# Second attention: the maxima of a pair's second head come between the turning of the next queries' first head and that of their second

## Chip, core and metric

The kernel runs on one core of one Trainium2 chip. The metric is the device time of one execution, in microseconds (us). Twelve runs of the kernel before gave a median of 2171.01 us (2167.87 to 2173.53).

## What is computed

Two layers in sequence over x of 16 x 256 tokens by 256 features, float32, each step followed by a residual add and a layer norm: an RWKV-like attention, a quantised gated feed-forward, a latent attention with rotary positions (the "second attention"), and a mixture of 32 experts. The change lies in the second attention, of which this is the core:

```
cq = rms_norm(x @ w_qa.T, q_a_ln_w)
q = (cq @ w_qb.T)                      # 16 heads, 128 + 64 features; the 64 are rotated
ckv = x @ w_kva.T                      # shared latent keys and values
scores = einsum('bhqd,bhkd->bhqk', q_full, k_full) * scale
scores = where(causal, -inf, scores)
attn = softmax(scores, axis=-1)
out = einsum('bhqk,bhkd->bhqd', attn, v)
return out @ w_o.T
```

The mixture's router (scores, group choice, top 4 of 32, places in the experts' slots) is worked out inside the second attention's time, on the same engines.

## The kernel before, in words

The tokens are cut into 8 blocks of 512 (two sequences each). In the second attention (lines 1050 to 1340) each block b has 8 steps p, one for each pair of heads; n = 8b + p counts them. All engines follow the order in which the Python code issues instructions (`manual_schedule`): each engine has its own in-order queue, and an instruction waits on semaphores for what it reads and for the buffer that it overwrites.

One turn of the loop at line 1267 works on three pairs at once: pair n+2 is *asked* (its queries are projected and rotated), pair n+1 is *scored* (scores, softmax), and pair n-1 is *seen* (probabilities turned keys first, contexts). In the order of the code:

- scores of the scored pair's first head (line 1108, two sequences, TensorE), their maxima (`maxima`, line 1119, VectorE, from PSUM into `sm`), their exponentials (`exps`, line 1132, ScalarE);
- the reciprocal (line 1143, VectorE) and the scaling of the probabilities (line 1145, GpSimd) of the second head of the pair before it;
- `queries` (lines 1072 and 1078, TensorE): two PSUM tiles `q_ps`, one for each head of the asked pair;
- `first_place`: router parts of an earlier block (lines 888 to 997, VectorE above all) in steps 5, 6, 7 and 0, a layer norm's last part in step 3;
- reciprocal and scaling of the scored pair's first head; then `keys_first` of sequence 0 (line 1158, transposes on TensorE; line 1162, copies `aT` on ScalarE, which stand behind the exponentials in ScalarE's queue);
- `turn` for both heads of the asked pair (lines 1083 to 1091): three VectorE products out of `q_ps` (lines 1087, 1088, 1089) and a GpSimd addition (line 1090);
- a scatter of router rows (line 1004, GpSimd queue);
- scores of the scored pair's second head (TensorE), contexts of sequence 0 (line 1171), `keys_first` of sequence 1;
- the maxima of the scored pair's second head (VectorE);
- another scatter, then `second_place`: router parts (steps 3 to 7, 0 and 1), parts of the next block's latents (lines 672 to 746), and in steps 1, 2, 5 and 6 `output` (line 1190, TensorE, with the residual add of line 1198);
- the exponentials of the second head, contexts of sequence 1, the copy `cT` (line 1333), a last scatter.

Two pools of PSUM buffers matter. `ps_s` holds the scores in 2 buffers (tag "s"), so the first head's scores of the next turn need the buffers that the second head's maxima read. `ps_m` holds 3 buffers (tag "m") that go round in the order of allocation: in each turn the two `q_ps` first, then the tiles of `first_place` and `second_place` (`l_ps`, `n_ps`, `xT_ps`, `lat_ps`, `cqT_ps`, `kT_ps`, `o_ps`), so that the third tile behind a `q_ps` takes that `q_ps`'s buffer. `turned` goes round three buffers, one for each head.

Of the kernel before, what the change touches and what calls it, by code (L numbers as in the profile page):

```python
# [88 lines left out]
def seq_postln_kernel(ctx: ExitStack, tc: tile.TileContext, a: dict, out: bass.AP, cap: int):  # L89
# [80 lines left out]
    def layernorm(ys, dsts):  # L170
        normalize(ys, dsts, *moments(ys))
# [827 lines left out]
    def scatter(b, which):  # L999


        dest = dests[b]
        for t, k in [divmod(j, K) for j in which]:
            put = nc.gpsimd.indirect_dma_start(  # L1004
                out=xp_d[:, :],
                out_offset=bass.IndirectOffsetOnAxis(ap=dest[:, k, t : t + 1], axis=0),
                in_=xs[b][:, t, :],
                in_offset=None,
                bounds_check=slots - 1,
                oob_is_err=False,  # L1010
            )
            if scattered:
                tc.declare_no_dep(put.ins, group="scatter", reason="other rows")
            tc.add_to_no_dep_group("scatter", put.ins)
            scattered.append(put.ins)
# [34 lines left out]
    with ExitStack() as ph:  # L1050
# [16 lines left out]
        def queries(cqT, pair):  # L1067

            pss = []
            for k in range(2):  # L1070
                ps = ps_m.tile([P, BLK], F32, tag="m", name="q_ps")
                nc.tensor.matmul(  # L1072
                    ps, lhsT=w_q[:, 2 * pair + k, :], rhs=cqT[:, 0, :], start=True, stop=False
                )
                pss.append(ps)
            for k, ps in enumerate(pss):
                rows = slice(k * QR, (k + 1) * QR)
                nc.tensor.matmul(
                    ps, lhsT=w_qr[rows, pair, :], rhs=cqT[rows, 1, :], start=False, stop=True
                )  # L1080
            return pss

        def turn(ps, h):
            qT = pq.tile([P, BLK], F32, tag="qT", name="qT")
            qr = turned[h % 3]
            lo, hi = slice(KVLR, KVLR + HR), slice(KVLR + HR, P)
            nc.vector.tensor_tensor(qT, ps, cst["q_cos"], ALU.mult)  # L1087
            nc.vector.tensor_tensor(qr[lo, :], ps[hi, :], cst["q_sin"][hi, :], ALU.mult)  # L1088
            nc.vector.tensor_tensor(qr[hi, :], ps[lo, :], cst["q_sin"][lo, :], ALU.mult)  # L1089
            nc.gpsimd.tensor_tensor(qT, qT, qr, ALU.add)  # L1090
            return qT
# [60 lines left out]
        def keys_first(heads, s):  # L1152

            aTs = []
            for sm in heads:
                a_ps = ps_a.tile([P, 3 * P], F32, tag="a", name="a_ps")
                for i in range(3):
                    nc.tensor.transpose(  # L1158
                        a_ps[:, i * P : (i + 1) * P], sm.pr[:, s, i * P : (i + 1) * P], ident
                    )  # L1160
                aT = pa.tile([P, 3 * P], F32, tag="aT", name="aT")
                copy = nc.scalar.copy(aT, a_ps)  # L1162
                aTs.append(aT)
            return aTs, copy

        def contexts(c_ps, aTs, copy, kf, s):


            for i in range(2):
                for k, aT in enumerate(aTs):  # L1170
                    mm = nc.tensor.matmul(  # L1171
                        c_ps[k * KVLR : (k + 1) * KVLR, s, i * P :],
                        lhsT=kf[:, 2 * s + i, :KVLR],
                        rhs=aT[:, : 2 * P] if i == 0 else aT[:, 2 * P :],
                        start=(i == 0),
                        stop=(i == 1),
                    )
                    if i == k == 0:
                        after(mm.ins, copy.ins, "beside the other head's")
# [32 lines left out]
        def step_latents(b):  # L1212
            if b < NB:
                if b not in lats:
                    lats[b] = latents(b, ps_m, "m")
                next(lats[b], None)

        def step_route(b):
            if b >= 0:
                if b not in routes:  # L1220
                    routes[b] = route(b, ps_m, "m")
                next(routes[b], None)

        def first_place(b, p):
            last = b - 1
            if p == 3 and last >= 0:
                x = x_t[last * NTT : (last + 1) * NTT]
                normalize(x, x, *norms.pop(last), eng=nc.scalar)
            if p >= 5:
                step_route(last)  # L1230
            if p == 0:
                step_route(last - 1)
# [25 lines left out]
        def scatters(b, p):  # L1258

            lo = 3 * (p - 2)  # L1260
            return [(b, j) for j in range(max(lo, 0), min(lo + 3, GT * K))] if b >= 0 else []

        NS = NB * NP
        with tc.manual_schedule(engines=engines):
            qTs, sms = {}, {}
            step_latents(1)
            for n in range(-2, NS + 1):
                b, p = divmod(n, NP)
                todo = scatters(b - 2, p)

                def one_scatter():
                    if todo:
                        scatter(todo[0][0], [todo.pop(0)[1]])

                scored = n + 1 if 0 <= n + 1 < NS else None
                asked = n + 2 if 0 <= n + 2 < NS else None
                seen = n - 1 if 0 <= n - 1 < NS else None
                if scored is not None:
                    kT = latent[scored // NP][2]
                    heads = sms[scored] = [Softmax(), Softmax()]  # L1280
                    qT2 = qTs.pop(scored)
                    for s in range(2):
                        heads[0].scores(qT2[0], kT, s)
                        heads[0].maxima(s)
                        heads[0].exps(s)
                if n in sms:
                    sms[n][1].divide()
                if asked is not None:
                    q_ps = queries(latent[asked // NP][0], asked % NP)
                if n >= 0:  # L1290
                    first_place(b, p)
                elif n == -2:

                    for _ in range(3):
                        step_latents(1)
                if scored is not None:
                    heads[0].divide()
                if seen is not None:
                    pair = sms.pop(seen)
                    kf = latent[seen // NP][1]  # L1300
                    part, j = divmod(seen % NP, NP // 2)
                    if j == 0:
                        cT = cTs[seen // NP, part] = pc.tile(
                            [P, NP // 2, BLK], F32, tag="cT", name="cT"
                        )
                    c_ps = ps_c.tile([P, 2, S], F32, tag="c", name="c_ps")
                    aTs0 = keys_first(pair, 0)
                    if p == 4:
                        step_latents(b + 1)
                if asked is not None:  # L1310
                    qTs[asked] = [turn(ps, 2 * asked + k) for k, ps in enumerate(q_ps)]
                one_scatter()
                if scored is not None:
                    heads[1].scores(qT2[1], kT, 0)
                    heads[1].scores(qT2[1], kT, 1)
                if seen is not None:
                    contexts(c_ps, *aTs0, kf, 0)
                    aTs1 = keys_first(pair, 1)
                if scored is not None:
                    heads[1].maxima(0)  # L1320
                    heads[1].maxima(1)
                one_scatter()
                if n >= 0:
                    second_place(b, p)
                elif n == -1:
                    for _ in range(2):
                        step_latents(1)
                if scored is not None:
                    heads[1].exps(0)
                    heads[1].exps(1)  # L1330
                if seen is not None:
                    contexts(c_ps, *aTs1, kf, 1)
                    nc.scalar.copy(cT[:, j, :], c_ps.rearrange("p s t -> p (s t)"))
                one_scatter()
            step_route(NB - 2)
            last = NB - 1
            for s in range(2):
                output(last, 1, s)
            x = x_t[last * NTT :]
            layernorm(x, x)  # L1340
# [298 lines left out]
```

## Time and profile before

| what | value |
| --- | --- |
| median of 12 runs | 2171.01 us |
| profiled execution, its own time | 2173.98 us |
| profiled execution, span of instructions | 2172.2 us |
| mean granted TensorE clock | 0.985 |
| busy: TensorE products / VectorE / ScalarE / GpSimd | 2077.4 / 1560.4 / 762.3 / 897.7 us |
| second attention, from about 1128 to about 1890 us | |
| from 1500 to 1600 us: TensorE / VectorE / ScalarE / GpSimd busy | 96.79 / 85.64 / 60.54 / 66.91 us |
| one block in the steady part (step 1 of block 4 to step 1 of block 5) | 1529.19 to 1626.60 us |

The time of the profiled execution is 1.8 us above its span, and 3 us above the median. PE stands for TensorE's products, PEld for its weight loads, DVE for VectorE, ACT for ScalarE, POOL for GpSimd. A timeline row has the start, the time, the engine, the line, the operation, its tiles, and in brackets the idle time of the engine just before it and what ended it. A row of the chain of waits has a start, a time and the instruction that held the end at that moment.

### The profile page before, as it was taken

Reading aid. Unit: us, or ns where it says so; the run is one execution under the profiler, and the core shown is the slowest. Engines: PE = TensorE matmul, PEld = TensorE weight load, DVE = VectorE, ACT = ScalarE, POOL = GpSimd, SP = SyncE. Lnnn points to the kernel's source line nnn. Section 1 sums busy time; section 2 is a strip of 40 time slices with the busy share of each in tenths; the row PEclk is TensorE's granted clock in tenths of the full one; section 3 lists DMA queues with packets and bytes.
Section 4 is the critical chain, followed back from the end, with each engine's and each line's share of the span. In section 5 each row is a group of like instructions: output and inputs, shape, how many; then the busy total and the mean of one; then the engine's idle time right before and its main releaser. Section 6 shows DMA issues by size and latency. Waiting matters only on the chain.

```text
span 2172.2 us, 29585 instructions
## 1 busy us (share of the span) xinstructions
PE 2077.4 (96%) x9544; PEld 1449.7 (67%) x9544; DVE 1560.4 (72%) x3960; ACT 762.3 (35%) x2237; POOL 897.7 (41%) x972
## 2 busy tenths in 40 slices
PE   8999999999999999999998999999999999988887
PEld 5777777777777777565555666666666666656665
DVE  7888888888888887223346679888797978853436
ACT  2212121211112112212225565656666564522323
POOL 5623232323232322000015545757666675734556
PEclk9999999999999999999999999999999999989999
DMA  9544444444453231110000000000000000042337
GB/s 314 183 133 148 129 136 131 140 130 148 135 151 95 88 95 49 48 34 1 0 1 1 1 1 1 29 4 6 3 4 2 3 3 2 25 169 66 88 134 294
DMA packets 102042, 169.73 MB, mean 78 GB/s; under 512 B 17807, under 2 KB 67191, under 8 KB 99712
## 3 DMA queue, kind: packets, MB, share of 16 engines
q1 hardware_dynamic: 88000, 158.45, 23.1%
q0 software_dynamic: 9216, 5.19, 0.9%
q10 hardware_dynamic: 4672, 4.21, 0.6%
q8 instruction: 76, 1.25, 0.2%
q14 instruction: 78, 0.64, 0.1%
HBM read 128.75 MB, written 56.95 MB: 85 GB/s over the span
## 4 chain that ended last, share of the span: by engine, by line
PE 71%; DVE 18%; ACT 4%; issue 2%; POOL 2%; DMA 1%; another core or an unknown queue 1%; POOLq 0%; SPq 0%; DVEq 0%; ACTq 0%
PE p_ps L419 15%; PE o_ps L512 10%; PE v_ps L449 8%; PE g_ps L208 4%; PE u_ps L208 4%; PE s_ps L1108 4%; PE d_ps L247 3%; PE o_ps L1190 3%; PE q_ps L1072 3%; PE c_ps L1171 3%; DVE sm L1119 2%; PE a_ps L1158 2%; DVE turned L1089 2%; DVE qT L1087 2%; DVE turned L1088 2%
## 5 line engine op out<-in xcount | busy, mean ns | idle before, releaser
L499 POOL TENSOR_TENSOR wkv<-su,Wr_sb 128x512 f32<-128x512 f32 x128 | 160.2, 1273 | 503.2 <-PE p_ps L419 313.9
L1145 POOL TENSOR_TENSOR pr<-pr,rr 128x256 f32<-128x256 f32 (+1 forms) x256 | 206.9, 836 | 153.9 <-DVE rr L1143 127.2
L512 PE MATMUL o_ps<-w_o,wkv 128*128 128x256 f32 (+1 forms) x1024 | 251.6, 388 | 6.2 <-POOL wkv L499 5.8
L1132 ACT ACTIVATE pr<-sm,nm 128x128 f32<-128x128 f32 (+1 forms) x512 | 226.1, 444 | 77.7 <-DVE nm L1119 63.4
L449 PE MATMUL v_ps<-xm,w_Wv 128*128 128x512 f32 x512 | 242.5, 596 | 6.0 <-DVE xm L395 6.0
L512 PEld LDWEIGHTS o_ps<-w_o,wkv 128*128 128x128 f32 x1024 | 192.1, 190 | 75.8 <-POOL wkv L499 45.1
L1108 PE MATMUL s_ps<-kT,qT 128*128 128x128 f32 (+1 forms) x1024 | 199.2, 338 | 22.2 <-DVE nm L1119 22.1
L421 ACT COPY t_sb<-p_ps 128x256 f32<-128x256 f32 x128 | 47.4, 370 | 467.2 <-PE p_ps L419 465.9
L419 PE MATMUL p_ps<-xm,w_Wk 128*128 128x256 f32 x896 | 204.9, 380 | 1.5 <-DVE Wr_sb L424 1.5
L419 PEld LDWEIGHTS p_ps<-xm,w_Wk 128*128 128x128 f32 x896 | 170.8, 191 | 52.9 <-issue 27.8
L419 PE MATMUL p_ps<-xm,w_Wr 128*128 128x256 f32 x896 | 204.4, 379 | 0.7 <-POOL xm L401 0.5
L1090 POOL TENSOR_TENSOR qT<-qT,turned 128x512 f32<-128x512 f32 x128 | 162.8, 1274 | 89.1 <-DVE turned L1089 87.9
L419 PEld LDWEIGHTS p_ps<-xm,w_Wr 128*128 128x128 f32 x896 | 170.0, 190 | 25.2 <-DVE Wk_sb L424 0.9
L1108 PEld LDWEIGHTS s_ps<-kT,qT 128*128 128x128 f32 x1024 | 146.8, 194 | 43.1 <-issue 35.4
L1162 ACT COPY aT<-a_ps 128x384 f32<-128x384 f32 x256 | 109.9, 481 | 170.6 <-PE a_ps L1158 170.4
L470 DVE TENSOR_TENSOR_SCAN st<-decay,kv 128x255 f32<-128x255 f32 x256 | 163.9, 682 | 4.4
L1119 DVE CUSTOM_DVE_ANT_0 sm<-s_ps,const 128x128 f32<-128x128 f32 (+1 forms) x512 | 154.2, 354 | 14.6 <-PE s_ps L1108 11.6
L1004 POOL DMA_INDIRECT xp_d<-xs,dest x128 | 128.3, 1002 | 58.8 <-issue 31.6
L142 POOL TENSOR_TENSOR rstd<-rs_t,nhalf 128x4 f32<-128x4 f32 (+1 forms) x33 | 33.3, 1010 | 287.3 <-DVE rs_t L141 277.1
L494 ACT ACTIVATE Wr_sb<-Wr_sb 128x512 f32<-128x512 f32 x128 | 73.5, 621 | 217.9 <-DVE Wr_sb L427 188.7
L449 PEld LDWEIGHTS v_ps<-xm,w_Wv 128*128 128x128 f32 x512 | 97.7, 191 | 74.3 <-issue 61.3
L218 DVE TENSOR_TENSOR hT<-sg,u_ps 128x512 f32<-128x512 f32 x56 | 38.4, 687 | 147.4 <-PE u_ps L208 134.0
(189 smaller groups left out, 3765.1 us busy)
## 6 DMA issues: line engine op xcount, KB each, us to landing
w_Wk<-wsum_d SPq DMA_DIRECT2D x56, 448.0 KB
w_Wr<-wsum_d SPq DMA_DIRECT2D x56, 448.0 KB
w_Wv<-in_Wv_dram SPq DMA_DIRECT2D x64, 256.0 KB
res_d<-zeros SPq DMA_DIRECT2D x16, 1024.0 KB
res<-res_d SPq DMA_DIRECT2D x16, 1024.0 KB
w_e<-in_W_experts_dram SPq DMA_DIRECT2D x32, 384.0 KB
xp_d<-empty SPq DMA_DIRECT2D x4, 1360.0 KB
xe<-xp_d SPq DMA_DIRECT2D x32, 170.0 KB
```

The source lines that it names most:

```text
L208: mm = nc.tensor.matmul(ps, lhsT=w[:, c, i * P : (i + 1) * P], rhs=xT[:, c, :], start=(c == 0), stop=(c == DC - 1),)
L419: nc.tensor.matmul(to, lhsT=w[:, at, :], rhs=x[:, bt, :], start=True, stop=True)
L449: nc.tensor.matmul(ps, lhsT=self.w3["Wv"][:, 2 * h + c, :], rhs=self.xms["Wv"][:, 2 * c : 2 * c + 2, :].rearrange("p s t -> p (s t)"), sta ...
L470: nc.vector.tensor_tensor_scan(st[:, s, 1:], decay[:, n : n + 1].to_broadcast([P, S - 1]), kv[:, s, : S - 1], 0.0, ALU.mult, ALU.add,)
L499: nc.gpsimd.tensor_tensor(wkv, self.su[h], self.both(self.r, h), ALU.mult)
L512: nc.tensor.matmul(ps.rearrange("p t d -> p (t d)") if opens else ps[:, tt % 2, :], lhsT=self.wkv[h][:, tt * P : (tt + 1) * P], rhs=w_o[:, ...
L1004: put = nc.gpsimd.indirect_dma_start(out=xp_d[:, :], out_offset=bass.IndirectOffsetOnAxis(ap=dest[:, k, t : t + 1], axis=0), in_=xs[b][:, ...
L1090: nc.gpsimd.tensor_tensor(qT, qT, qr, ALU.add)
L1108: nc.tensor.matmul(ps[:, lo:hi], lhsT=qT[:, s * S + i * P : s * S + (i + 1) * P], rhs=kT[:, s * S : s * S + hi - lo], start=True, stop=True,)
L1119: nc.vector.tensor_tensor_reduce(out=sm[:, lo:hi], in0=self.ps[s][:, lo:hi], in1=cst["mask"][:, lo:hi], scale=-(DQ**-0.5), scalar=-MASKED, ...
L1132: nc.scalar.activation(self.pr[:, s, lo:hi], self.sm[s][:, lo:hi], AF.Exp, bias=self.nm[:, s, i : i + 1], scale=-1.0, accum_out=self.rs[:, ...
L1145: nc.gpsimd.tensor_tensor(self.pr[:, :, lo:hi], self.pr[:, :, lo:hi], rr[:, :, i : i + 1].to_broadcast([P, 2, hi - lo]), ALU.mult,)
```

## The change

In the turn of the loop, the second head of the asked pair is turned after the maxima of the scored pair's second head, where it was turned before them.

```diff
                 if asked is not None:
-                    qTs[asked] = [turn(ps, 2 * asked + k) for k, ps in enumerate(q_ps)]
+                    qTs[asked] = [turn(q_ps[0], 2 * asked)]
                 one_scatter()
                 if scored is not None:
                     heads[1].scores(qT2[1], kT, 0)
                     heads[1].scores(qT2[1], kT, 1)
                 if seen is not None:
                     contexts(c_ps, *aTs0, kf, 0)
                     aTs1 = keys_first(pair, 1)
+
                 if scored is not None:
                     heads[1].maxima(0)
                     heads[1].maxima(1)
+                if asked is not None:
+                    qTs[asked].append(turn(q_ps[1], 2 * asked + 1))
                 one_scatter()
```

No instruction is added or taken away. TensorE, ScalarE and SyncE keep their order. On VectorE the second head's lines 1087 to 1089 pass behind the four maxima (line 1119); on GpSimd the second head's addition (line 1090) passes behind one scatter (line 1004), in the steps that have one.

## Prediction

> **What bounds the kernel now.** I read the page first, then the sums by stretch, the waits of TensorE inside the second attention (1128 to 1890 us), the chain of waits over one steady block, and the timelines of the engines over that block. TensorE is busy 96.8% of the stretches from 1400 to 1800 us and VectorE 85.6%, so what TensorE waits for there is short:
>
> ```profile
> PE s_ps L1108 <- DVE nm L1119: 22.1, 14, 5.3
> PE c_ps L1171 <- ACT aT L1162: 9.1, 13, 0.8
> ```
>
> The columns are the total, the number of waits and the longest. The scores wait for the maxima that still read their buffer: that is the wait the change aims at. In a steady block it comes twice, in the turn's first scores of step 0 and of step 1:
>
> ```profile
> 1613.45 0.87 PE L1171 MATMUL c_ps<-aT,kf 128*64 128x256 f32 x8
> 1615.76 1.55 PE L1108 MATMUL s_ps<-kT,qT 128*128 128x128 f32 x8 [1.45 <-DVE nm L1119]
> ...
> 1626.60 1.55 PE L1108 MATMUL s_ps<-kT,qT 128*128 128x128 f32 x8 [0.91 <-DVE nm L1119]
> ```
>
> The chain of waits over the block says why: from step 4 on it holds nothing but VectorE rows, until the maxima let TensorE go.
>
> ```profile
> 1572.51 0.18 DVE rr L1143
> ...
> 1626.11 0.34 DVE sm L1119
> 1626.47 0.14 issue
> 1626.60 1.55 PE s_ps L1108 x8
> ```
>
> So from 1572.5 to 1626.5 VectorE sets the pace and never idles; afterwards TensorE does (steps 1 and 2), with a turn through ScalarE in step 3. An order that only shuffles VectorE's work gains at the one place where the chain leaves VectorE, and loses whatever makes VectorE's own work longer.
>
> **What moving the turn gains.** A turn is 0.71 us three times, 2.13 us (from 1623.68 to 1625.81). Behind the maxima it no longer delays the release of the scores' buffers: -2.13 us, once a block, at the exit in step 0. In steps 4 to 7 it gains nothing, because VectorE does the turn anyway before the next maxima.
>
> **What it costs on VectorE.** GpSimd's addition (line 1090, 1.27 us) starts 0.15 us behind its turn. Until now the second head's addition ran beside the maxima, which read one operand from PSUM and one from SBUF; after the change it runs beside the router's parts of `second_place`, whose products have both operands in SBUF. What that does shows in the rows:
>
> ```profile
> 1510.07 1.93 DVE L866 TENSOR_TENSOR eq<-left,top 128x128 f32<-128x128 f32 x1
> 1510.22 1.62 POOL L1145 TENSOR_TENSOR pr<-pr,rr 128x256 f32<-128x256 f32 x2
> ...
> 1537.97 1.28 POOL L1090 TENSOR_TENSOR qT<-qT,turned 128x512 f32<-128x512 f32 x1 [0.90 <-DVE turned L1089]
> 1538.97 0.31 DVE L984 COPY pos<-carry 128x32 f32<-128x32 f32 x1
> ...
> 1589.42 1.28 POOL L1090 TENSOR_TENSOR qT<-qT,turned 128x512 f32<-128x512 f32 x1 [0.86 <-DVE turned L1089]
> 1590.42 0.56 DVE L866 TENSOR_TENSOR gt<-gs 128x256 f32<-128x256 f32 x1
> ...
> 1595.45 1.66 POOL L1145 TENSOR_TENSOR pr<-pr,rr 128x256 f32<-128x256 f32 x2 [1.03 <-DVE top L952]
> 1595.47 0.73 DVE L866 TENSOR_TENSOR eq<-left,top 128x128 f32<-128x128 f32 x1
> 1596.24 1.01 DVE L866 TENSOR_TENSOR eq<-eq,const 128x128 f32<-128x128 f32 x1
> ```
>
> The comparison `eq`, 0.29 us at its quickest, takes 1.93, 0.73 or 1.01 us beside a GpSimd product, and always ends about 0.15 us behind it. The last two groups beside line 1090 show that the addition does the same: the copy and `gt` last until just behind its end. With T the end of the second turn, the addition holds VectorE's SBUF products until T + 1.42. Step by step:
> - Step 4: line 909 comes first, at T + 0.03, 0.12 us ahead of the addition. If it is held, it ends at T + 1.5 and not at T + 0.3: 1.2 us. If it gets through, the addition starts behind it and holds line 717 for about 0.25 us. Below these the bound is nothing. The nearest row is 1510.07, an operation 0.15 us ahead that was held: 1.2 us.
> - Step 5: `gt` ends at T + 1.7 where it would take 0.42 us: 1.23, less the 0.13 that it already loses: 1.1 us.
> - Steps 6 and 7: a reduction runs first (not held), then `eq` ends at T + 1.57 where it would end at T + 0.52: 1.05 us each.
> - Step 7 gets something back: the 1.93 us came with both halves of line 1145 back to back behind a scatter. VectorE being later, GpSimd is idle by then, and the pair becomes 0.73 + 1.01, as in step 6: -0.47 us.
>
> At the exit: 1.2 + 1.1 + 1.05 + 1.05 - 0.47 - 2.13 = +1.8 us. TensorE starts step 1 that much later, since the 2.36 us that it waited are all the slack it had.
>
> The Trainium skill, "SBUF — State Buffer", section "Who interferes with whom", says that a VectorE instruction with two SBUF inputs contends with a GpSimd one that reads SBUF, and that whichever issues first has the ports for its whole length. The second half speaks for line 909 in step 4, and the row at 1510.07 against it. By the rule step 4 costs 0.25 us, the exit comes at +0.85 us, and the whole sum is some 6 us smaller.
>
> **What it costs on TensorE.** The moved turn is also the last reader of the second `q_ps`, and its buffer of three comes back later by the maxima, 1.2 us.
> - Step 3: `lat_ps` is the third tile behind it and starts at 1565.92; the turn would end at 1566.35 where it ended at 1565.12. TensorE waits 0.46 us, and line 691, its reader, stands in the chain: +0.46 us.
> - Step 1: `o_ps` is the third tile (behind `n_ps` and `lat_ps`). Before, the turn ended at 1537.82 and `o_ps` started at 1538.60, one block later 1635.2 and 1636.0. Now VectorE enters the step with the turn of step 0 still to do (2.13) and two small copies held by its addition (0.35): its first maxima start at 1628.06 + 1.8 + 2.48 = 1632.3. From there to the reciprocal of line 1143 it is 2.27 us as before (ScalarE's exponentials); the copies `aT` stand behind these and end at 1635.45, 0.7 us after TensorE wants them. Turn, maxima, turn from 1634.7: 2.13 + 1.2 + 2.13, ends at 1640.15. `o_ps` arrives at 1636.0 + 1.8 + 0.7 = 1638.5 and waits for that: TensorE is now 4.15 us late. In step 2 VectorE's idle time (0.9, 0.95 and 2.79 us before) takes up its lag.
> - Step 0's first `q_ps` also waits for the turn of step 7, some 1.2 us, but the contexts behind it wait longer for `aT`: nothing more.
>
> ScalarE's exponentials of the second head are free sooner but stand behind the copies: nothing. The scatter that passes ahead, and the second query itself, used half a turn later, have some 5 us to spare: nothing.
>
> **The sum.** A block: 4.15 + 0.46 = 4.6 us. Blocks 1 to 5: 23.0. Block 6 (step 1 of block 7 has no `lat_ps`, so `o_ps` takes another buffer; TensorE waits there at a lower clock already): an estimate from the parts above, 0.46 + 1.5 = 2.0. Block 7 has only steps 4 and 5, partly hidden: 1.6. Block 0 has no router parts and TensorE sets its pace: nothing. In the very first turns the maxima release earlier (-2.13) but the addition now stands ahead of line 142 (+1.15): -1.0. Together +25.6 us: the span of the profiled execution would go from 2172.2 to 2197.8, and the median, 3 us below that execution's own time, from 2171.0 to 2196.6. With step 4 at 0.25 it is 2190.6.
>
> **Rivals.**
> - GpSimd's addition costs VectorE nothing (the moved pairs don't meet, or short operations slip through). Then the exit gains 2.13 us, but in step 1 the turn ends at 1635.95 whatever happened before, since the exponentials set it, and `o_ps` starts within 0.1 us of where it did: +0.4 a block with step 3. Blocks 1 to 5 give +2.0, block 6, without that wait, -4.5, the first turns -1: 2167.5 us. Against it: the rows above, in every block.
> - Faster, the other side: neither the addition nor the buffer of `q_ps` binds, and the waits for the maxima vanish: 22.1 us less the two of the first turns (5.3 and 2.85) is 13.95; the 3.1 us of the low clock behind the 1.86 us wait at 1810.58 (2.90 for 1.55, 3.62 for 1.88); and 1.0 at the start: -18, 2153 us. It decides if the second turn ends before the third tile behind `q_ps` is due in steps 1 and 3; now that margin is 0.8 us in both, and the turn moves by 1.2.
> - The new waits in steps 7 and 0 (up to 1.8 us at once) bring the low clock each block: in the stretch 1810 to 1818 us, behind waits of 0.68 and 1.86 us, the granted clock was 0.58; behind 1.45 us it stayed at 1.00. Six times 3.1 us on top: 2215 us.
> - That the order does not change can be left out: on VectorE and GpSimd it is as the diff says, on the other engines as before.
>
> **Numbers.** Forecast 0.68 (its own range 2180 to 2208), low clock 0.08, no cost beside the addition 0.14, faster 0.10. Slower by over 0.2% (2175.4 us; about what a measurement of this kernel can tell from no change): 0.76. The third case straddles the band: 0.10 within, 0.04 faster; with the last, faster 0.14. The range runs from 2163, which takes in the third case, to the low clock's 2215.
>
> **What would show it.** Right: `eq` of steps 6 and 7's `second_place` and `gt` of step 5 at 1.3 to 1.7 us beside line 1090; VectorE's waits unchanged but its busy time up by some 25 us; TensorE waiting at `o_ps` in step 1 and `lat_ps` in step 3 for line 1089; a block of about 102 us. Wrong: `eq` at 0.29 us there; or TensorE's first scores of step 1 earlier in the block than now; or a block of 95 us.

## The result and the profile after

The changed kernel takes 2189.49 us (median of 7 runs, 2187.05 to 2193.72) against 2169.75 us for the kernel before on the same chip (28 runs): a ratio of 1.0093, 95% interval 1.0084 to 1.0103, so +19.7 us. The forecast was 2196.6. The profiled execution of the changed kernel takes 2187.3 us, its span is 2185.5.

TensorE's order is the same in both kernels, so the two traces can be laid side by side, from step 1's first scores of one block to those of the next. A steady block takes 100.79 us after and 97.41 before: +3.38, where the forecast said +4.6. Taken by steps (from a step's first scores to those of the next), step 1 is 1.79 us longer, step 3 0.47, steps 4 to 0 together 1.12 (1.04 of it in step 0), and the others are the same. The attention's last contexts start 17.7 us later.

TensorE's waits inside the second attention, after (total, number, longest):

```profile
PE s_ps L1108 <- POOL qT L1090: 16.7, 9, 7.9
PE c_ps L1171 <- ACT aT L1162: 15.1, 25, 0.8
PE o_ps L1190 <- DVE turned L1089: 7.5, 5, 1.5
PE xT_ps L179 <- DVE turned L1089: 6.1, 5, 1.2
PE s_ps L1108 <- DVE nm L1119: 1.7, 1, 1.7
PE lat_ps L684 <- DVE turned L1089: 1.2, 6, 0.2
```

The wait for the maxima (nm), which the change aims at, has all but gone: 22.1 us became 1.7. Its place is taken by other waits for VectorE's turns (o_ps, xT_ps, lat_ps) and, in the scores themselves, by a wait for GpSimd's addition. The longest of these, 7.9 us, stands in the very first turns, where the maxima cost 5.3 and 2.9 us before. TensorE's timeline shows where in the block the others stand; the last row is from before, where o_ps came without a wait:

```profile
1725.76 0.66 PE L179 MATMUL xT_ps<-const,xs 128*128 128x128 f32 x4 [1.22 <-DVE turned L1089]
...
1727.19 1.58 PE L1108 MATMUL s_ps<-kT,qT 128*128 128x128 f32 x8
...
1739.07 1.58 PE L1108 MATMUL s_ps<-kT,qT 128*128 128x128 f32 x8 [0.94 <-POOL qT L1090]
...
1750.16 3.72 PE L1190 MATMUL o_ps<-w_ov,cT 128*128 128x256 f32 x16 [1.49 <-DVE turned L1089]
...
1636.01 3.62 PE L1190 MATMUL o_ps<-w_ov,cT 128*128 128x256 f32 x16
```

The first four are step 7, step 0's first scores (their wait of 1.45 us is gone), step 1's first scores and step 1's o_ps. The chain of waits no longer leaves VectorE at step 1's scores as it did before. It stays on VectorE, with one turn through ScalarE's exponentials, up to o_ps:

```profile
1740.88 1.05 DVE sel L973
...
1742.80 1.87 ACT pr L1132 x8
...
1749.42 0.70 DVE turned L1089
...
1750.16 3.72 PE o_ps L1190 x16
```

So whatever lengthens VectorE's work in steps 4 to 7 now also sets o_ps. And VectorE's work did get longer. The timeline of all engines, at the second turns of steps 4, 5 and 6 and at step 7's first part; the last two rows are from before, the same products of steps 5 and 7:

```profile
1689.36 0.23 DVE L909 TENSOR_SCALAR sco<-sco 128x128 f32<-128x128 f32 x1
1689.42 1.31 POOL L1090 TENSOR_TENSOR qT<-qT,turned 128x512 f32<-128x512 f32 x1 [0.51 <-DVE turned L1089]
...
1701.94 0.42 DVE L866 TENSOR_TENSOR gt<-gs 128x256 f32<-128x256 f32 x1
1702.06 1.43 POOL L1090 TENSOR_TENSOR qT<-qT,turned 128x512 f32<-128x512 f32 x1 [0.81 <-DVE turned L1089]
1702.28 1.49 DVE L866 TENSOR_TENSOR eq<-gs 128x256 f32<-128x256 f32 x1
...
1716.04 1.26 POOL L1090 TENSOR_TENSOR qT<-qT,turned 128x512 f32<-128x512 f32 x1 [0.82 <-DVE turned L1089]
1716.24 1.21 DVE L866 TENSOR_TENSOR eq<-left,top 128x128 f32<-128x128 f32 x1
...
1720.88 0.73 DVE L866 TENSOR_TENSOR eq<-left,top 128x128 f32<-128x128 f32 x1
1721.64 1.01 DVE L866 TENSOR_TENSOR eq<-eq,const 128x128 f32<-128x128 f32 x1
...
1688.31 0.41 DVE L866 TENSOR_TENSOR eq<-gs 128x256 f32<-128x256 f32 x1
1713.81 0.29 DVE L866 TENSOR_TENSOR eq<-left,top 128x128 f32<-128x128 f32 x1
```

A product out of two SBUF operands that is caught by the addition lasts until just behind the addition's end: `eq` 1.49 us where it took 0.41, and 1.21 where it takes 0.29. In the step 4 pair nothing is caught. To put a number on it, I add up in one block what VectorE's operations last over the shortest time of their kind in the steady blocks of all traces, as far as that is more than 0.1 us: 3.7 us before and 6.0 to 6.3 after.

### The profile page after: what moved, and what is told of

It is laid out like the page before. It is cut to its first block, busy times and chain, and to the rows that moved or that the text cites. A ratio compares the mean times of both kernels' runs of the same rounds, so it can differ in the third digit from the quotient of the medians.

```text
span 2185.5 us, 29567 instructions
## 1 busy us (share of the span) xinstructions
PE 2070.9 (95%) x9544; PEld 1441.6 (66%) x9544; DVE 1576.3 (72%) x3960; ACT 758.1 (35%) x2237; POOL 898.6 (41%) x972
## 4 chain that ended last, share of the span: by engine, by line
PE 67%; DVE 24%; issue 3%; ACT 3%; POOL 2%; another core or an unknown queue 1%; DMA 0%; POOLq 0%; DVEq 0%; ACTq 0%; SPq 0%
PE p_ps L419 15%; PE o_ps L512 10%; PE v_ps L449 8%; PE g_ps L208 4%; PE u_ps L208 4%; DVE sm L1119 3%; PE s_ps L1108 3%; PE d_ps L247 3%; PE o_ps L1190 3%; DVE eq L866 2%; DVE turned L1089 2%; DVE turned L1088 2%; PE c_ps L1171 2%; DVE qT L1087 2%; PE q_ps L1072 2%
## 5 line engine op out<-in xcount | busy, mean ns | idle before, releaser
L1108 PE MATMUL s_ps<-kT,qT 128*128 128x128 f32 (+1 forms) x1024 | 197.5, 336 | 18.4 <-POOL qT L1090 16.7
```

The source lines that it names most:

```text
L1108: nc.tensor.matmul(ps[:, lo:hi], lhsT=qT[:, s * S + i * P : s * S + (i + 1) * P], rhs=kT[:, s * S : s * S + hi - lo], start=True, stop=True,)
```

## The experiments

Two theories stood against each other in what follows. Theory 1: the late addition on GpSimd stands beside the router's products and lengthens VectorE's chain. Theory 2: the second q_ps's buffer comes back late, and TensorE waits for it at o_ps. The runs were made on several chips. They differ mainly behind the attention: from its last contexts to the end of the span it is 267 us in the trace of the changed kernel, 231 in b_late's. Each run is therefore compared with the kernel before on its own chip, and the steady block, which does not contain that part, is compared across all of them.

### The addition cut short, in the new order and in the old

```diff
-            nc.gpsimd.tensor_tensor(qT, qT, qr, ALU.add)
+            nc.gpsimd.tensor_tensor(qT[:, :cols], qT[:, :cols], qr[:, :cols], ALU.add)
...
-                    qTs[asked].append(turn(q_ps[1], 2 * asked + 1))
+                    qTs[asked].append(turn(q_ps[1], 2 * asked + 1, 16))
```

> The order of after, with the second head's addition on GpSimd (line 1090) cut from 512 columns to 16: it leaves the rotation's second part out of the other columns, so that GpSimd no longer holds VectorE's ports for 1.3 us behind the late turn, while the late turn itself and the late return of the second q_ps stay. Theory 1 (the addition beside the router's products is what costs): the 1.07 us of step 5 and the 0.93 us of steps 6 and 7 vanish, the time falls from 2189 to within 3 us of the kernel before or below it (2160 to 2173 us). Theory 2 (the late return of q_ps costs): o_ps in step 1 still waits for line 1089, and the time stays above 2182 us. If both share it: about 2175 to 2180 us.

> The control for the run before: the order of before, with the same addition cut to 16 columns (the same part of the rotation is left out). Beside the maxima the addition cost VectorE next to nothing, so both theories expect the time of before, 2166 to 2170 us; if it is far lower, the addition's length matters by itself (through the scores that wait for it), and the pair has to be read by its difference.

Both kernels leave the rotation's second part out of all but 16 columns of the second head. The new order came to 2130.59 us, the old one to 2126.40, before to 2131.12 on that chip: ratios of 0.9996 (0.9987 to 1.0005) and 0.9981 (0.9972 to 0.9990). A block takes 97.47 us in the new order and 96.46 in the old. Against the whole addition, the new order has lost 3.32 us a block and the old one 0.95. The control was expected to stay where it was and did not: beside the old neighbours the addition was not free either (in the control `gt` takes 0.42 us where it took 0.56 before, and the slow `eq` of step 7 takes 0.72 where it took 1.93), so the pair is read by its difference. The addition's length costs 2.4 us a block more in the new order than in the old. That is theory 1, but not all of it: with the addition short in both, the new order is still 1.0 us a block slower than the old, and o_ps in step 1 still waits 1.2 us for line 1089.

### The addition alone moved

```diff
+                if asked is not None:
+                    qT, qr = adds[0]
+                    add = nc.gpsimd.tensor_tensor(qT, qT, qr, ALU.add)
+                    if scored is not None:
+                        after(add.ins, last_max.ins, "behind the maxima")
```

> The order of before on VectorE and TensorE, both turns ahead of the maxima; only the second head's addition on GpSimd waits for the last maximum, so that it stands beside the router's products as in after. q_ps comes back as early as before, and the maxima release the scores' buffers as late as before. Theory 1: VectorE's chain from step 4 to step 0 grows by 1.07 + 0.93 + 0.93 us a block (and up to 0.7 more in step 7), about 3 us a block over six blocks: 2184 to 2192 us. Theory 2: nothing but the later second query, 2169 to 2174 us.

2152.58 us against 2131.12: a ratio of 1.0100 (1.0084 to 1.0115), +21.5 us, and a block of 99.92 us (+2.5). No VectorE or TensorE instruction has moved, and the kernel is about as slow as with the whole change. Its block shows the addition's price better than its time does: in b_late's trace the granted clock falls to half at five places between 1327 and 1833 us, for 3.4 to 6.8 us each, and two of its blocks take 100.9 and 101.6 us; in the trace of the changed kernel it does so nowhere between 1157 us and the attention's end. The rows are the same as after, step 6 in the timeline of all engines:

```profile
1715.44 1.26 POOL L1329 TENSOR_TENSOR qT<-qT,turned 128x512 f32<-128x512 f32 x1 [0.95 <-DVE nm L1122]
1715.51 1.33 DVE L866 TENSOR_TENSOR eq<-left,top 128x128 f32<-128x128 f32 x1
```

VectorE's operations last 6.5 us over their shortest in the block, against 3.7. TensorE pays at the exit, where the first scores of steps 0 and 1 wait for the maxima; step 1's wait grew from 0.91 to 1.96 us:

```profile
1727.94 1.55 PE L1111 MATMUL s_ps<-kT,qT 128*128 128x128 f32 x8 [1.45 <-DVE nm L1122]
...
1739.83 2.27 PE L1111 MATMUL s_ps<-kT,qT 128*128 128x128 f32 x8 [1.96 <-DVE nm L1122]
```

### Step 1's o_ps in another buffer

```diff
-            ps = ps_m.tile([P, BLK], F32, tag="m", name="o_ps").rearrange("p (k d) -> p k d", k=2)
+            ps = pool.tile([P, BLK], F32, tag=tag, name="o_ps").rearrange("p (k d) -> p k d", k=2)
...
-                output(last, 1, p - 1)
+                output(last, 1, p - 1, *((ps_a, "a") if p == 1 else ()))
```

> After, with the o_ps of step 1 taken from the pool of the transposed probabilities (ps_a), whose buffer is free by then, in place of the buffer of the second q_ps: TensorE's wait of 1.49 us for line 1089 in step 1 goes. Theory 2: 1.5 us in each of five blocks go, 2180 to 2183 us. Theory 1: TensorE meets VectorE's lag a little later, at most 3 us of it go, 2186 to 2190 us.

> The control for the run with o_ps in the other pool: the order of before, with the o_ps of step 1 taken from ps_a. Before had no wait at o_ps, so both theories expect no change, within 2 us of before and a block of 97.4 us; a gain here would mean that the other pool helps by itself.

In the new order: 2142.16 us, a ratio of 1.0050 (1.0037 to 1.0064) to before, where the change as it stands has 1.0093; a block of 99.02 us, 1.77 less. The line of o_ps is gone from TensorE's waits and the others stay:

```profile
PE s_ps L1108 <- POOL qT L1090: 15.9, 9, 7.9
...
PE xT_ps L179 <- DVE turned L1089: 6.1, 5, 1.2
```

The control in the old order: 2168.41 us against 2168.15, a ratio of 1.0004 (0.9995 to 1.0013), a block of 97.41. The other pool helps nothing by itself. Theory 2 is right too: at o_ps the buffer costs 1.8 us a block, and its whole wait was on the path. At lat_ps in step 3 it costs 0.47 us more: step 3 is longer by that much in each run whose step 3 has the late turn, with the whole addition or the short one, this run too. It is not longer at all in b_late and in the two runs below that keep the old order there.

### The new order in some steps only

```diff
-                    qTs[asked] = [turn(q_ps[0], 2 * asked)]
+                    late = n >= 0 and p == 0
+                    qTs[asked] = [turn(q_ps[k], 2 * asked + k) for k in range(1 if late else 2)]
...
-                if asked is not None:
+                if asked is not None and late:
                     qTs[asked].append(turn(q_ps[1], 2 * asked + 1))
```

In the other two runs, `late` is true in steps 7 and 0, and in steps 1 to 6 and the first turns.

> The new order in step 0 of each block alone; the other steps keep the order of before. Both theories: step 0 has no product out of two SBUF operands behind its late turn but two small copies (0.28 us), and its tiles are too few for the second q_ps's buffer to bind. The wait of 0.91 us at the first scores of step 1 goes (TensorE is ready 0.91 us earlier, the first head's addition ends 1.5 us earlier): a block of 96.5 us instead of 97.41, and 5 to 6 us less than before in all. If the first scores of step 1 then wait for something else, nothing changes.

> The new order in steps 7 and 0 alone. Contention: 0.93 us at eq in step 7, behind the release that step 0 waits for. Gain: the wait of 1.45 us in step 0 goes, and the first scores of step 1 come 1.47 us behind the first turn of step 0, where they came 2.95 us behind it, because the addition of that turn now ends last. Together 0.5 to 1 us a block: 3 to 7 us less than before. If the late return of q_ps in step 7 (xT_ps waits 1.2 us) is on the path: no gain, within 2 us of before.

> The complement: the new order in steps 1 to 6 and in the first two turns, that of before in steps 7 and 0. Contention: 1.07 us in step 5 and 0.93 in step 6 lengthen VectorE's chain, with no release gained at the exit: a block of 99.4 us, +12 to +14 us in all. If the buffer alone were the cause, step 1 (where VectorE is not behind by a turn any more, so that o_ps waits little) would show +0 to +4 us.

Step 0 alone: 2163.41 us against 2168.15, a ratio of 0.9978 (0.9969 to 0.9987), a block of 96.64 us. This is **faster than either kernel**. Step 0's first scores wait as before, step 1's no longer do:

```profile
1612.64 1.55 PE L1108 MATMUL s_ps<-kT,qT 128*128 128x128 f32 x8 [1.44 <-DVE nm L1119]
...
1622.50 1.58 PE L1108 MATMUL s_ps<-kT,qT 128*128 128x128 f32 x8
```

Steps 7 and 0: 2167.57 us, a ratio of 0.9997 (0.9988 to 1.0006), a block of 97.65 us. The expected 3 to 7 us did not come. The second case of the expectation did, but not for its reason: xT_ps does not wait for a turn in these blocks. Between first scores, step 7 is 1.51 us shorter (the wait in step 0 is gone), but step 0 is 1.04 longer: `eq` is held for 0.92 us, and step 1's scores now wait for the first head's addition. Step 1 is 0.71 longer, of which o_ps waits 0.42.

Steps 1 to 6: 2186.81 us, a ratio of 1.0080 (1.0066 to 1.0095), +18.7, a block of 99.9 us. It is dearer than expected (+12 to +14), mainly because the expectation left out what the late buffer costs. By steps, step 7 is 1.5 us longer, steps 1 (o_ps) and 3 (lat_ps) 0.46 each. VectorE's operations are held for 1.1 us more than before; the rest of step 7's 1.5 lies in small gaps between operations whose neighbours changed. In the block this run has 2.5 of the change's 3.38 us and the one before it 0.24. The missing 0.6 is at o_ps in step 1: it costs 0.46 and 0.71 us in these two runs and 1.79 when every turn is late.

### What the gain would be without either cost

The new order with the short second addition and o_ps in ps_a, then with the first head's addition short too, and the old order with both short:

```diff
-            nc.gpsimd.tensor_tensor(qT, qT, qr, ALU.add)
+            nc.gpsimd.tensor_tensor(qT[:, :16], qT[:, :16], qr[:, :16], ALU.add)
```

> The new order with both costs taken away: the second head's addition cut to 16 columns (the second part of the rotation is left out of the rest) and the o_ps of step 1 in ps_a. What is left is the gain at the exit, against 96.46 us a block in the order of before with the same short addition. If the gain is the whole turn, as forecast (2.13 us): 94.3 us a block. If the first head's addition now ends last at the first scores of step 1 (it ends 1.47 us behind its turn, where the scores came 2.95 us behind it), the gain is at most about 1 us: 95.5 to 95.8 us a block.

> The same with the first head's addition cut to 16 columns too. If that addition is what clips the gain at the first scores of step 1, these come 0.8 us earlier (the maxima ended 0.85 us ahead of it), and a block takes 94.7 to 95.0 us. If it is not, the block stays within 0.2 us of the run with the whole first addition.

> The control: the order of before with both additions cut to 16 columns. There the maxima end last, not the first addition: a block of 96.4 us, as with the second addition alone cut. If it falls as much as the run of the new order with both cut, the first addition costs by its length in either order, and nothing is shown about the clipped gain.

The times: 2158.48, 2154.04 and 2161.80 us against 2168.33, ratios of 0.9956 (0.9941 to 0.9971), 0.9935 (0.9920 to 0.9950) and 0.9965 (0.9952 to 0.9979). The blocks: 96.01, 95.68 and 96.47 us. With the short second addition and the other buffer the new order gains 0.45 us a block over the old with the same short addition (96.46). That is what is left of 1.0 us gained at the exit (steps 7 and 0), since step 3 still takes 0.48 us longer, where lat_ps waits for its buffer. So the gain at the exit is half of the 2.13 forecast. The first scores of step 1 show why. In the first of these runs:

```profile
1717.08 1.58 PE L1108 MATMUL s_ps<-kT,qT 128*128 128x128 f32 x8 [0.72 <-POOL qT L1090]
```

The maxima have let the buffer go, but the query itself is not there: its turn stands just ahead of these maxima, and GpSimd's addition ends 1.4 us behind the turn. With that addition short too, the wait is gone:

```profile
1714.11 0.87 PE L1171 MATMUL c_ps<-aT,kf 128*64 128x256 f32 x8
1715.06 1.55 PE L1108 MATMUL s_ps<-kT,qT 128*128 128x128 f32 x8
```

TensorE now comes straight from its contexts. The scores start 0.65 us earlier against the turn, nearly what the wait said (0.72), but the block is only 0.33 shorter: 0.34 us comes back inside step 1. I take it that this is because VectorE has the late turn still to do there; no run shows it. The control did not move (96.46 to 96.47), so it is not the addition's length as such. My expectation of 94.7 to 95.0 left out what comes back.

### A version put together from these

The new order in all steps but 3 and the first turns, o_ps in ps_a, and the late addition behind the router's last product of its step:

```diff
+                    for qT, qr in adds if asked is not None else ():
+                        add = nc.gpsimd.tensor_tensor(qT, qT, qr, ALU.add)
+                        if "tt" in last_of:
+                            after(add.ins, last_of["tt"], "behind the router")
```

> A whole kernel put together from what the runs showed: the new order in all steps but step 3 and the first two turns; o_ps of step 1 in ps_a; and the late head's addition waits for the router's last product of second_place, so that it stands beside the residual add and the maxima, which read PSUM. If contention and buffer are the two costs, and the second query has half a turn to spare: a block of 95.8 to 96.5 us, 6 to 10 us less than before. If the deferred addition comes too late for the second head's scores, or holds the parts of first_place or the scaling of the probabilities instead: no better than the new order in step 0 alone, 96.6 us or more.

A miss: 2173.47 us, a ratio of 1.0023 (1.0014 to 1.0032), a block of 98.8 us. The timeline of all engines shows it holding other operations instead. In step 4 it meets the four scalings of line 717, which take 0.77 us at their quickest:

```profile
1679.80 2.54 DVE L717 SCALAR_TENSOR_TENSOR kf<-lat,rms,kv_ln 128x64 f32<-128x64 f32 x4
1680.76 1.29 POOL L1333 TENSOR_TENSOR qT<-qT,turned 128x512 f32<-128x512 f32 x1
```

And the scaling of the probabilities comes later behind it and catches more of first_place:

```profile
1710.68 1.92 DVE L866 TENSOR_TENSOR eq<-eq,const 128x128 f32<-128x128 f32 x1
1710.82 1.62 POOL L1148 TENSOR_TENSOR pr<-pr,rr 128x256 f32<-128x256 f32 x2
```

VectorE's operations are held for 7.4 us a block, more than after. An addition is not free merely because it has left the products that it was seen to hold.

## Why the prediction was right, and where its sizes were off

The direction and both mechanisms hold, and each is shown by a run of its own: the addition beside the router's products by a run that has it alone (b_late, +2.5 us a block; 2.4 as the difference of the pairs), the late buffer by one that takes it away at o_ps (a_ops, 1.8). The short additions split the change into 2.37 for the addition (3.32 - 0.95), 1.46 for o_ps's buffer (97.47 - 96.01) and -0.45 for the gain less lat_ps's wait. That these add up to +3.38 proves nothing, since each run is the start of the next difference. The steps do test the forecast, term by term: 1.12 us for the exit (steps 4 to 0), 1.79 for step 1 and 0.47 for step 3, where it said 1.8, 2.35 and 0.46.

**The cost on VectorE** was forecast as 1.2 + 1.1 + 1.05 + 1.05 - 0.47 = 3.9 us a block; the rows of the same operations give 0.03 + 0.68 + 0.92 + 0.92 - 0.48 = 2.1.
- Step 4 is the step that failed. "The nearest row is 1510.07, an operation 0.15 us ahead that was held: 1.2 us." That row is a product with two operands in SBUF; line 909 adds a constant to one. It ran in 0.23 us, 0.06 us ahead of the addition and 0.10 less than before, and line 717 lost 0.13. The alternative by the skill's rule gave 0.25 for this step. The sum made with it, 2190.6 us, is nearly the measured median, partly because the next two errors cancel.
- Step 5: 1.07 us, on `eq` and not on `gt`, which got through with a lead of 0.12. Line 938, which lost 0.25 before, and `gt`, which lost 0.14, are free now: 0.7 in all against 1.1.
- Steps 6 and 7: 0.92 each against 1.05. The pair of step 7's first part came as forecast (0.73 + 1.01), worth -0.48. The copy of line 974 loses 0.28 (forecast 0.35 for two copies).

**The gain at the exit**, -2.13 us, was over-sized: with the short additions it is 1.0. (2.1 less 1.0 is the 1.1 us by which steps 4 to 0 are longer.) I looked at when the maxima release the buffer and not at when the next operand of the waiting product is there. The first head's addition, which ends 1.4 us behind its turn, was 1.5 us early before and is late by 0.94 after.

**The cost on TensorE** at o_ps was forecast as 4.15 us late in all: 1.8 from the exit and 2.35 inside step 1. Inside step 1, o_ps came 1.68 us later (1739.07 to 1750.16, against 1626.60 to 1636.01). VectorE's first maxima stood 3.33 us behind step 1's scores, against 1.46 before: 1.87 later and not 2.48, because the scores had themselves waited for the addition. The two sizes belong together: what the exit does not gain, o_ps does not wait for. lat_ps in step 3 waits 0.20 us, and the step is 0.47 longer, as forecast (0.46).

**The sum.** Up to step 1 of block 2 the traces are 1.4 us apart (forecast 3.6: -1.0 for the first turns and 4.6), over the next four blocks 13.6 (18.4), in block 6 1.6 (2.0), in block 7 up to the last contexts 1.0 (1.6). Together that is the 17.7 us at the last contexts. Behind them the two profiled executions differ by 4.4 us the other way, at granted clocks of 0.95 after and 0.91 before, so these traces do not show where the rest of the medians' 19.7 lies.

**What was to be seen.** Seen: `eq` at 1.2 to 1.5 us beside line 1090, o_ps and lat_ps waiting for line 1089, a block of about 102 us (100.8). Not seen: VectorE busy 25 us longer (15.9), and step 0's first q_ps waiting for the turn of step 7. What waits in step 7 is the second xT_ps, 1.22 us, for the first turn of the same step. It waits in b_late too, where no q_ps is late: it is VectorE's lag, not the moved turn.

**The rivals.** "GpSimd's addition costs VectorE nothing" falls with b_late. "Faster" falls for the change as a whole; its point of decision, the margin of 0.8 us at o_ps, was one of two: step 0, which has neither such a tile nor a router product behind its late turn, alone gains 0.77 us a block. The low clock did not come: the mean granted clock is 0.992 after and 0.985 before, and block 6, which took 99.14 us before behind its dip, took 100.78 after like the others. In b_late it did come.

## What to carry to other kernels

Before moving an operation, follow everything that it triggers: here the moved products return a buffer later, and the addition that another engine starts behind them holds the products that now stand there. Each costs some 2 to 2.5 us a block. A release that comes earlier is worth only as much as the next of the waiting instruction's operands allows, so list all its operands with their times, not only the one that the profile names. And a reordering inside a loop need not be made in every turn: in the one step where the wait stands and no cost falls, it gains 0.2%, and made everywhere it loses 0.9%.

## What the runs showed of the hardware

Which of the two engines gets through is not told by the recorded starts alone. `gt`, with a lead of 0.12 us over an addition, ran at full speed, and the addition took 1.43 us where it takes 1.27. `eq` at 1710.68 in the last run, with a lead of 0.14, was held to 1.92 us. Line 909 got through with 0.06, but it reads only one tensor (not that this makes it safe: before, where it began while an addition was running, it took 0.33 us for 0.23 and ended 0.1 us behind it). The Trainium skill, "SBUF — State Buffer", section "Who interferes with whom", says of VectorE's two-port mode that whoever issues first gets the shared ports for the whole instruction, and of contention in general that issue order decides who blocks. By the recorded starts, that fits `gt` and not `eq`.

In the case of `eq`, GpSimd's product came straight behind a scatter; ahead of `gt`, GpSimd had been idle for 0.81 us, waiting for the turn. That is not the whole answer either. In the first turns of the changed kernel, line 717 stands 0.05 us ahead of an addition for which GpSimd had waited 1.97 us, and its four scalings, 0.77 us at their quickest, took 1.98:

```profile
1154.90 1.98 DVE L717 SCALAR_TENSOR_TENSOR kf<-lat,rms,kv_ln 128x64 f32<-128x64 f32 x4
1154.94 1.26 POOL L1090 TENSOR_TENSOR qT<-qT,turned 128x512 f32<-128x512 f32 x1 [1.97 <-DVE turned L1089]
```

No run here separates these causes.
